# Two transformer blocks on one core: ScalarE makes the statistics of the first batches' normalizations and evicts the conditioning, the first batches get due times of their own, and two unread products run first

## The chip, the core and the metric

The kernel runs on one core of a Trainium2 chip. A core has TensorE (matrix products, "PE" in the profile), VectorE ("DVE"), ScalarE ("ACT"), GpSimd ("POOL") and SyncE ("SP", which here only issues DMAs). Each engine runs its own instructions strictly in the order in which they were written, and waits at semaphores for the others. The metric is device microseconds of one execution. Before the change the median of 3 runs is 1350.14 us (1349.22 to 1350.87).

## The reference

There are 16 batches of 256 tokens with 256 channels, all in fp32. Every batch goes through two blocks; the shapes in brackets are those of one batch.

```
c = silu(cond)                                   # per batch, 256
m = c @ w_ada + b_ada                            # 9 rows of 256: shift, scale, gate, three times
# block 0
h = ln(x) * (1 + m1) + m0;  q, k, v = split(h @ w_qkv + b_qkv)
    attention in two windows of 128, rolled by 64, 16 heads of 16       -> x += (o @ w_so + b_so) * m2
h = ln(x) * (1 + m4) + m3;  q = h @ w_q + b_q;  k, v = split(ctx @ w_kv + b_kv)
    scores 256 x 256 a head; the 16 largest of each row alone are kept,
    softmax over them                                                   -> x += (o @ w_co + b_co) * m5
h = ln(x) * (1 + m7) + m6;  a, b = split(h @ w_m1 + b_m1)               # 1024 each
    x += ((silu(a) * b) @ w_m2 + b_m2) * m8
# block 1
q from ln(x) * (1 + s1) + t1,  k, v from ln(ctx) * (1 + s2) + t2, where s, t = c @ Wss + bss
    attention over 256 keys                                             -> out = x + o @ Wp + bp
```

`ln` subtracts the mean of a row of 256 and divides by the root of its variance (with an epsilon). A batch has five of them: before the self attention, the top-k attention and the feed forward part (on x), and two in the last block, on the context and on x. What the change touches is how `ln`'s mean and variance are made for some batches, which engine takes the conditioning (m, s, t) out of the matrix product, and the order of everything.

## The kernel before, in words

Tokens lie on the 128 partitions, so that a batch is two tiles of 128 x 256. The pieces of a batch carry tags: `self` (self attention), `prep` (the context's keys and values and the queries for the top-k attention), `topk` (the top-k attention in four rounds of 4 x 2 heads), `mlp` and `last`; what is made once, such as weights, biases and conditioning, is tagged `start`.

Nothing runs in the order of the source. Each helper records operations with `op(engine, cost, emit, ...)`, that is, with the buffers that they read and write. Every operation has a due time: its batch plus an entry of the table `DUE` divided by 1000. The entry is found by the tag and by a running number within the tag. Tags of the first and the last batches have a number of their own (`self0`, `prep1`, `mlp15`), where that table entry stands for one batch alone; `self`, `prep`, `topk`, `mlp` and `last` serve all others. `Plan.order` sorts all operations by due time, assigns buffers, and writes the instructions out in this order, so a single list sets the order on all engines and on the DMA queue. It also estimates times from the given costs, with which it decides one thing: where TensorE would stand idle for over 1 us it puts in `filler` products (L353), one to two products of the identity that nobody reads.

The steps that the change touches:

- `normalized` (L436): VectorE makes the statistics with two `bn_stats` and two `bn_aggr` (L442, L444), GpSimd makes the reciprocal root and the negated mean in three small operations (L449 to L451), and then the normalized tile in two (L454). TensorE turns the result (L466), and ScalarE scales and shifts it while it copies it out (L480).
- `ada_columns` (L714): a piece of a weight of 256 KB is loaded (`rest<-in_L_xcond_w_ada_dram`, L711), multiplied with the conditioning (L721), and VectorE adds the bias from `bcol` as it copies the product out (L727, L729: two instructions of 128x16). There are 10 such pieces.
- `topk_round`: four score banks (L845), on each of which VectorE runs `max`, `match_replace`, `max`, `match_replace` for two heads (L864, L872, L884, L889), ScalarE the exponentials (L877), GpSimd the product of both (L893); then TensorE turns the weights (L542) and multiplies them with the values (L598).
- `lower`: 16 DMAs of 1 KB (L622) bring the negated maxima into the queries before the second scores (L806, L962).

The stationary layouts of TensorE differ: 128 x 128 for the big products, 32 rows at a time for the scores, and 17 columns for the weighted values (L598).

Of the kernel before, what the change touches and what calls it, by code (L numbers as in the profile page):

```python
# [10 lines left out]
F32 = mybir.dt.float32  # L11
# [5 lines left out]
P = 128  # L17
# [17 lines left out]
        -9079, -9474, -9247, -7795, -10959, -5686, -7231, -10933, -5595, -5764, -7671, -10944, -8055, -6777, -10987,  # L35
        -8081, -7859, -719, -437, -438, -481, -6999, -7280, -511, -720, -536, -6808, -436, -8602, -467, -7346, -144,
        -528, -1472, -8696, -179, -78, -9103, -26, -462, -493, -574, -8606, 35, 199, -2104, 292, -47, 992, 1098, 1338,
        -644, 26, -8994, -144, 52, 10, -8772, -241, -8701, 551, 74, 19, 1012, -516, -8708, 29, 1085, 1257, -514, -452,
        -6996, 1627, 1833, 1607, 911, 1468, 582, -843, -8601, 1445, 486,
    ),  # L40
    "self0": (
        -199, -1161, -7107, -1119, -1199, -1060, -1485, -9186, -125, -11006, -9245, -9080, -1563, -9248, -3868, -1470,
        -9200, -1606, -6831, -7277, -7299, -7349, -1217, -6958, -8697, -6883, -8698, -8665, -312, -310, -2158, -3486,
        -3338, -3035, -3750, -1684, -9048, -7290, -1182, -7290, -2158, -3339, -3752, -3826, -3561, -128, -8903, -9100,
        -1236, -8924, 9, -4022, -51,
    ),
    "prep0": (
        -524, -3251, -614, -3532, -3488, 354, -2949, 516, -8780, -39, -37, 80, 196, -3410, 569, -100, -3471,
    ),
    "topk0": (  # L50
        338, 282, 143, 7, -2799, -24, 100, -98, -2853, -35, 73, -8610, -2853, -8623, 112, -8616, -3052, -8436, -261,
        148, 579, -3006, -8621, -8749, 142, 439, -2809, 383, 324, 558, 726, -3356, -8631, -8719, 484, 172, -2951, 700,
        959, 1002, 919, 1061, 392, -8453, 550, -8714, -3364, 156, -461, 619, -3499, -8620, 551, 18, -2986, -61, 600,
        525, 700, 764, 725, 748, 690, -3352, 906, 842, 826, 553, 724, -72, 621, 835, 742, -3579, 803, 913, 816, 1073,
        821, 1081, 1074, 1309, 1219, 1329, 523, 620, 786, 1012, -3363, 1018, 801, 909, -3366, 958, 747, 1071, -3580,
        914, 791, 1170, -3634, 1022, 1024, 929, 1074, 820, 1013, 1016, 882, 1086, 819, 1181, 1178, 1255, 1240, 907,
        1133, 1169, 1256, 1239, 356, 1199, 1303, 1172, 1160, 1328, 1014, 1043, 1101, 1277, -3653, 1038, 1200, 1248,
        409, 1104, 1256, 1284, 352, 1060, 1143, 1107, 820, 1126, 1125, 1086, 972, 1307, 1262, 1260, 1197, 1206, 350,
        1052, 1246, 1188, 1311, 44, 1162, 1262, 1203, 1208, 1113, 1319, 1173, 1303, 1217, 1329, 677, 1356, 1398, 1437,
    ),  # L60
    "self1": (
        -4802, -987, -890, -482, -9103, -2047, -2146, -2225, -1549, -4844, -830, -1228, -5196, -3811, -1470, -4841,
        -4773, -861, -3828, -878, -800, -795, -794, -10252, -1021, -10208, -10029, -9854, -9854, -780, -807, -1214,
        -647, -4386, -4386, -4444, -3942, -602, -1053, -474, -328, -94, -659, -4237, -4066, -4401, -4387, -598, -1062,
        -270, -247, -15, 68, -4369, -213,
    ),
    "prep1": (
        -771, -5058, 71, -4579, -15, -331, -4364, 378, 34, 220, 223, 231, 182, -29, 145, 237, 302,
    ),
    "topk": (  # L70
        75, 3, 189, 110, 62, 3, -90, 2, 110, -39, 146, -53, -991, -146, 143, -62, -955, 353, 414, 558, 675, -104, 128,
        193, 253, 480, -914, 242, 339, 417, 490, -137, 393, 516, 407, 576, 134, 697, 349, 735, 402, 1049, 530, 279,
        443, -349, 556, 186, 562, 282, 1, 362, 587, 185, 11, 298, 611, 223, 479, 184, 179, 630, 712, -106, 253, 325,
        663, 746, 44, 673, 676, 706, 802, 580, 536, 739, 373, 857, 761, 882, 688, 894, 661, 942, 689, 837, 737, 833,
        885, 737, 799, 832, 902, 347, 344, 704, 30, 337, 331, 643, 725, 836, 941, 190, 1036, 1011, 826, 838, 232,
        1029, 960, 745, 776, 746, 903, 907, 736, 760, 415, 902, 909, 1090, 853, 1036, 1144, 1150, 894, 940, 677, 1028,
        721, 964, 206, 947, 922, 899, 675, 1026, 1075, 934, 678, 824, 918, 1039, 1051, 810, 1113, 1056, 691, 992, 779,
        1040, 959, 1033, 1027, 1116, 1109, 854, 1034, 1034, 999, 1107, 1008, 1160, 1027, 956, 1194, 1085, 501, 1236,
        1061, 1158,
    ),  # L80
    "self": (
        -1974, -677, -761, -758, -1718, -1767, -1387, -1242, -787, -1974, -758, -688, -1415, -1974, -694, -590, -601,
        -589, -1833, -538, -566, -1347, -1349, -1348, -345, -418, -466, -472, -473, -465, -226, -194, -253, -935,
        -969, -968, -425, -138, -335, -332, -197, -113, -150, -1139, -298, -295, -227, -133, -256, -227, -162, -70,
        -86, -126, -322,
    ),
    "prep": (
        -13, -197, -211, 5, 112, 57, 324, -19, -554, -568, -220, -220, -131, 617, 6, 17,
    ),
    "last": (  # L90
        1013, 1044, 1117, 1178, 1185, 1226, 6, 1311, 1060, 579, 1353, 1396, 2041, 1826, 1981, 1931, 2094, 1980, 2195,
        2146, 2088, 2131, 2195, 2090, 2231, 1173, 1171, 2258, 2182, 2188, 2187, 2280, 2286, 2324, 2285, 2351, 2342,
        2323, 2365, 2397, 2127, 2172, 2174, 2173, 2438, 2020, 2436, 1144, 1120, 1010, 1009, 2491, 2276, 2527, 2557,
        2522, 1882, 1284, 1283, 1388, 2589, 2220, 2310, 2627, 2557, 2593, 2591, 2133, 2518, 2425, 2647, 2528, 2649,
        2630, 2660, 2404, 2402, 2518, 2500, 2696, 2346, 2343, 2729, 2753, 2837, 2026, 2507, 2778,
    ),
    "mlp": (
        1668, 1326, 1271, 1268, 1484, 1490, 263, 1703, 1600, 1470, 1499, 1559, 1526, 1674, 1632, 1661, 1535, 959, 187,
        1556, 1289, 1565, 387, 1576, 1568, 1509, 398, 1568, 1257, 1602, 1505, 1616, 1614, 1238, 1421, 1717, 1041,
        1735, 1238, 1735, 1861, 1881, 1096, 1599, 1507, 1509, 1880, 1847, 1806, 859, 1648, 1897, 1712, 1861, 1529,  # L100
        1236, 1674, 882, 881, 1669, 1488, 1497, 847, 1474, 1745, 1088, 1027, 1748, 1027, 1396, 1020, 1336, 1944, 1978,
        1824, 2000, 1827,
    ),
    "self15": (
        -1762, -523, -14014, -616, -1736, -1651, -1652, -1042, -1147, -1738, -740, -1095, -1898, -709, -1266, -1267,
        -714, -1266, -347, -461, -328, -681, -998, -682, -328, -692, -173, -199, -712, -536, -370, -134, -249, -135,
        -196, -91, -162, -473, -302, -550, -648, -122, -354, -338, -167, -311, -83, -133, -766, -1659, -1733, -391,
# [1006 lines left out]
```

## Time and profile before

| what | value |
|---|---|
| median of 3 runs | 1350.14 us |
| profiled execution | 1350.46 us, its span 1348.6 us |
| PE busy | 1323.5 us (98%) |
| DVE busy | 1217.5 us (90%) |
| ACT busy | 1014.2 us (75%) |
| POOL busy | 1020.9 us (76%) |
| instructions in the span | 38673 |
| DMA | 42.45 MB, 31 GB/s in the mean |

The span runs from the first to the last instruction; the time holds some 1.9 us around it. The profile's windows give, for a stretch of the span, how long each engine was busy, the clock that TensorE was granted (1.00 is full speed) and what the DMA engines moved. A batch returns every 78.97 us in the middle of the span: the first score product of a top-k round of batches 3, 4 and 5 starts at 255.2, 334.2 and 413.2 us.

### The profile page before, as it was taken

Reading aid. Unit: us, or ns where it says so; the run is one execution under the profiler, and the core shown is the slowest. Engines: PE = TensorE matmul, PEld = TensorE weight load, DVE = VectorE, ACT = ScalarE, POOL = GpSimd, SP = SyncE. Lnnn points to the kernel's source line nnn. Section 1 sums busy time; section 2 is a strip of 40 time slices with the busy share of each in tenths; the row PEclk is TensorE's granted clock in tenths of the full one; section 3 lists DMA queues with packets and bytes.
Section 4 is the critical chain, followed back from the end, with each engine's and each line's share of the span. In section 5 each row is a group of like instructions: output and inputs, shape, how many; then the busy total and the mean of one; then the engine's idle time right before and its main releaser. Section 6 shows DMA issues by size and latency. Waiting matters only on the chain.

```text
span 1348.6 us, 38673 instructions
## 1 busy us (share of the span) xinstructions
PE 1323.5 (98%) x13494; PEld 1033.3 (77%) x13494; DVE 1217.5 (90%) x4358; ACT 1014.2 (75%) x2359; POOL 1020.9 (76%) x1552
## 2 busy tenths in 40 slices
PE   8889999999999999999999999999999999999998
PEld 6557787878778787887878788787878778787785
DVE  4699999999999999999999999999999999998844
ACT  4356779787887978778787777878777787978774
POOL 1377887879688787968878796887869788877962
PEclk9889999999999999999999999999999999999999
DMA  5430010101001010100101010010101000000000
GB/s 157 139 109 10 26 41 11 41 17 33 18 18 41 11 40 18 34 17 19 41 11 38 20 34 18 18 41 11 38 20 34 18 27 17 18 18 2 17 2 18
DMA packets 64161, 42.45 MB, mean 31 GB/s; under 512 B 37763, under 2 KB 56751, under 8 KB 63711
## 3 DMA queue, kind: packets, MB, share of 16 engines
q1 hardware_dynamic: 63967, 39.99, 10.7%
q8 instruction: 107, 1.75, 0.6%
q14 instruction: 87, 0.71, 0.2%
HBM read 35.14 MB, written 4.29 MB: 29 GB/s over the span
## 4 chain that ended last, share of the span: by engine, by line
PE 92%; DVE 3%; SPq 1%; issue 1%; DMA 1%; ACT 1%; POOL 0%; POOLq 0%; DVEq 0%; ACTq 0%
PE W L906 17%; PE W L492 12%; PE W L598 11%; PE W L542 8%; PE W L933 8%; PE W L528 6%; PE W L575 6%; PE W L950 5%; PE W L845 5%; PE W L962 5%; PE W L466 3%; PE W L806 2%; PE W L798 2%; SPq L622 1%; DVE rest L872 1%
## 5 line engine op out<-in xcount | busy, mean ns | idle before, releaser
L893 POOL TENSOR_TENSOR prT<-rest,prT 128x512 f32<-128x512 f32 x256 | 325.0, 1273 | 75.0 <-DVE rest L889 73.5
L605 DVE TENSOR_REDUCE nm<-W 128x2 f32<-128x512 f32 (+1 forms) x384 | 239.9, 682 | 30.9 <-PE W L798 17.4
L877 ACT ACTIVATE prT<-W,ntop 128x256 f32<-128x256 f32 x512 | 214.2, 491 | 52.2 <-POOL ntop L866 38.8
L906 PE MATMUL W<-xT,w_L_xcond_w_m 128*128 128x256 f32 (+1 forms) x1088 | 249.1, 373 | 0.0
L629 ACT ACTIVATE pTO<-W 128x512 f32<-128x512 f32 (+1 forms) x392 | 198.8, 596 | 41.9 <-PE W L962 28.9
L906 PEld LDWEIGHTS W<-xT,w_L_xcond_w_m 128*128 128x128 f32 x1088 | 187.6, 190 | 52.3 <-ACT pTO L629 10.6
L872 DVE MATCH_REPLACE8 rest<-top,W 128x256 f32<-128x256 f32 x512 | 209.0, 419 | 0.0
L889 DVE MATCH_REPLACE8 rest<-top,rest 128x256 f32<-128x256 f32 x512 | 206.7, 416 | 0.0
L864 DVE MAX8 top<-W 128x8 f32<-128x256 f32 x512 | 190.1, 420 | 15.7 <-PE W L845 12.8
L884 DVE MAX8 top<-rest 128x8 f32<-128x256 f32 x512 | 190.7, 418 | 0.0
L545 ACT ACTIVATE pTT<-W 128x512 f32<-128x512 f32 x256 | 148.7, 622 | 17.2 <-PE W L542 15.2
L542 PE MATMUL W<-ident,prT 128*128 128x128 f32 x1024 | 145.2, 277 | 4.4 <-ACT k L514 1.7
L542 PEld LDWEIGHTS W<-ident,prT 128*128 128x128 f32 x1024 | 117.9, 142 | 27.9 <-issue 6.2
L923 POOL TENSOR_TENSOR mb<-ma,mb 128x256 f32<-128x256 f32 (+1 forms) x136 | 94.8, 697 | 40.1 <-ACT mb L921 24.4
L558 POOL TENSOR_TENSOR on<-tr,rec 128x128 f32<-128x128 f32 (+1 forms) x162 | 71.0, 443 | 67.8 <-DVE rec L557 67.5
L933 PE MATMUL W<-w_L_xcond_w_m,h 128*128 128x256 f32 x512 | 113.7, 379 | 0.0
L933 PEld LDWEIGHTS W<-w_L_xcond_w_m,h 128*128 128x128 f32 x512 | 97.0, 190 | 13.7 <-POOL x L416 0.3
L555 DVE STREAM_TRANSPOSE tr<-W 128x256 f32<-128x256 f32 (+1 forms) x162 | 78.4, 485 | 29.6 <-PE W L598 15.6
L598 PE MATMUL W<-pTO,v 128*17 128x128 f32 (+1 forms) x2112 | 102.2, 323 | 0.0
L926 POOL TENSOR_TENSOR h<-h,mb 128x256 f32<-128x256 f32 (+1 forms) x136 | 94.7, 696 | 8.2
L416 POOL TENSOR_TENSOR x<-x,gated 128x512 f32<-128x512 f32 (+1 forms) x49 | 60.4, 1233 | 40.9 <-ACT gated L415 40.9
L921 ACT ACTIVATE mb<-W,half 128x256 f32<-128x256 f32 (+1 forms) x136 | 64.4, 489 | 31.7 <-PE W L906 31.6
(129 smaller groups left out, 2678.5 us busy)
## 6 DMA issues: line engine op xcount, KB each, us to landing
gate<-gates SPq DMA_DIRECT2D x48, 256.0 KB
q<-nmT SPq DMA_DIRECT2D x480, 1.0 KB
cx<-in_ctx_dram SPq DMA_DIRECT2D x19, 256.0 KB
cx<-in_ctx_dram SPq DMA_DIRECT2D x104, 32.0 KB
rest<-in_L_xcond_w_ada_dram SPq DMA_DIRECT2D x9, 256.0 KB
x<-in_x_dram SPq DMA_DIRECT2D x16, 128.0 KB
x<-in_x_dram SPq DMA_DIRECT2D x32, 64.0 KB
w_L_xcond_w_m<-in_L_xcond_w_m_dram SPq DMA_DIRECT2D x1, 2048.0 KB
```

What stands on the lines that cost most here:

```text
L542: nc.tensor.transpose(w.t[:, ts(n, P)], flat[:, ts(n, P)], ident)
L598: nc.tensor.matmul(po.t[ds(NW * j, DH + 1), ds(q0, nq)], v.t[:, kt, 8 * m + 2 * j + a, :], pT.t.rearrange("p n q -> p (n q)")[:, ds(part, ...
L605: op("DVE", 0.61, lambda j=j, s=s: nc.vector.tensor_reduce(nm.t[:, k, ds(j, groups, step=4)], s.t.rearrange("p (g k) -> p g k", g=groups), ...
L629: op("ACT", 0.24 + q * 0.0005, lambda s=s, pT=pT: nc.scalar.activation(pT.t.rearrange("p n q -> p (n q)")[:, :q], s.t[:, :q], AF.Exp), r=[ ...
L864: nc.vector.max(top.t[:, a, 0:8], s.t[:, ts(a, L)])
L872: nc.vector.match_replace(rest.t[:, a, :], top.t[:, a, 0:8], s.t[:, ts(a, L)], TAKEN)
L877: nc.scalar.activation(pr.t[:, a, :], s.t[:, ts(a, L)], AF.Exp, bias=ntop.t[:, a:a + 1])
L884: nc.vector.max(top.t[:, a, 8:16], rest.t[:, a, :])
L889: nc.vector.match_replace(rest.t[:, a, :], top.t[:, a, 8:16], rest.t[:, a, :], TAKEN)
L893: op("POOL", 1.25, lambda: nc.gpsimd.tensor_tensor(pr.t, rest.t, pr.t, ALU.mult), r=[rest, pr], w=[pr])
L906: nc.tensor.matmul(w.t[:, :q], w_m1.t[:, c, ds(n0, P)], xT.t[:, c, :q], start=c == 0, stop=c == NCC - 1)
L933: nc.tensor.matmul(pp.t[:, ts(k, C)], hs[f].t[:, ts(k, P)], w_m2.t[:, f, :], start=f == 0, stop=f == NHC - 1)
```

## The change

1. `normalized` gets a second way, `by_scalar`: ScalarE adds up each tile (an Identity into a tile `unread` with `accum_out`), GpSimd turns the sum into the negated mean, ScalarE squares with this mean as the bias and adds up again, and GpSimd makes the root. Seven normalizations take it: the self attention's and the top-k attention's of batches 1 and 2, and for batch 0 the feed forward's and both of the last block.
2. `ada_columns` has its products taken out by ScalarE. For the scales a second copy of the biases, `bcol1`, holds the bias plus one.
3. `self2`, `prep2`, `topk1`, `mlp0`, `mlp1`, `last0` and `last1` become tags of their own, and all due times are new.
4. Two products of a tile of ones (`warmed`), which nobody reads, stand first on TensorE. VectorE sets this tile as its first instruction, and makes the head masks a little later in the source.
5. The plan's DMA rate (`RATE`, in KB per us) is 250 instead of 320, which changes its estimates, and with them where fillers stand and which buffers are taken.

```
-ISSUE, BEGIN, LAND, RATE, OPEN = 0.53, 0.9, 0.4, 320.0, 8
+WARM = 2
+ISSUE, BEGIN, LAND, RATE, OPEN = 0.53, 0.9, 0.4, 250.0, 8
...
+    unread = const.tile([P, C], F32, name="unread")
...
+    nc.vector.memset(tiles["rest"][-1], 1.0)
...
+    def warmed():
+
+        z, w = tiles["rest"][-1].rearrange("p a l -> p (a l)"), tiles["W"][-1]
+        for _ in range(WARM):
+            nc.tensor.matmul(w, z[:, :P], z, start=True, stop=True)
...
-    def normalized(x, eps, tt):
-
-        st, mv, xn, n = Buf("st"), Buf("mv"), Buf("xn"), len(tt)
+    def normalized(x, eps, tt, by_scalar=False):
+
+
+        mv, xn, n = Buf("mv"), Buf("xn"), len(tt)
+        if by_scalar:
+            def added():
+                for k, t in enumerate(tt):
+                    nc.scalar.activation(unread, x.t[:, t, :], AF.Identity, accum_out=mv.t[:, k, 0:1])
+            op("ACT", 0.08 + 0.45 * n, added, r=part(x, tt), w=[mv])
+            op("POOL", 0.25, lambda: nc.gpsimd.tensor_scalar(mv.t[:, :n, 2], mv.t[:, :n, 0], -1.0 / C, None, ALU.mult), r=[mv], w=[mv])
+
+            def squares():
+                for k, t in enumerate(tt):
+                    nc.scalar.activation(unread, x.t[:, t, :], AF.Square, bias=mv.t[:, k, 2:3], accum_out=mv.t[:, k, 1:2])
+            op("ACT", 0.08 + 0.45 * n, squares, r=[*part(x, tt), mv], w=[mv])
+
+            def root():
+                m = mv.t[:, :n, 1]
+                nc.gpsimd.tensor_scalar(m, m, 1.0 / C, eps, ALU.mult, ALU.add)
+                nc.gpsimd.tensor_tensor(m, m, neg_half[:, :n], ALU.pow)
+            op("POOL", 0.8 + 0.16 * n, root, r=[mv], w=[mv])
+            return scaled(x, xn, mv, tt)
+        st = Buf("st")
...
-    bcol = fixed("bcol", [P, total])
+    bcol, bcol1 = fixed("bcol", [P, total]), fixed("bcol1", [P, total])
...
-        op("DVE", 0.2, lambda: nc.vector.tensor_copy(bcol.t[:, ds(first, total)], w.t[:, :total]), r=[w],
-           w=[(bcol, names is first_biases)])
+        def emit():
+            nc.vector.tensor_copy(bcol.t[:, ds(first, total)], w.t[:, :total])
+            nc.vector.tensor_scalar(bcol1.t[:, ds(first, total)], w.t[:, :total], 1.0, None, ALU.add)
+        op("DVE", 0.35, emit, r=[w], w=[(bcol, names is first_biases)])
...
-                if plus_one:
-                    nc.vector.tensor_scalar(dst.t[:, m, :], pm.t[:, ds(m * P, B)], col(bias, chunk + m), 1.0, ALU.add, ALU.add)
-                else:
-                    nc.vector.tensor_scalar(dst.t[:, m, :], pm.t[:, ds(m * P, B)], col(bias, chunk + m), None, ALU.add)
-        op("DVE", 0.32, out_of_it, r=[pm, cols(bias)], w=[dst])
+                c = col_of[bias] + chunk + m
+                nc.scalar.activation(dst.t[:, m, :], pm.t[:, ds(m * P, B)], AF.Identity, bias=(bcol1 if plus_one else bcol).t[:, c:c + 1])
+        op("ACT", 0.6, out_of_it, r=[pm, cols(bias)], w=[dst])
...
-        xT = channel_major(normalized(x, EPS0, tt), nt, 0, b)
+        xT = channel_major(normalized(x, EPS0, tt, b in (1, 2)), nt, 0, b)
...
-        xT = channel_major(normalized(x, EPS0, tt), len(tt), 1, b)
+        xT = channel_major(normalized(x, EPS0, tt, b in (1, 2)), len(tt), 1, b)
...
-        xT = channel_major(normalized(x, EPS0, tt), nt, 2, b)
+        xT = channel_major(normalized(x, EPS0, tt, b < 1), nt, 2, b)
...
-        cT = channel_major(normalized(load_cx(b), EPS1, BOTH), NT, "kv", b)
+        cT = channel_major(normalized(load_cx(b), EPS1, BOTH, b < 1), NT, "kv", b)
...
-        xT = channel_major(normalized(x, EPS1, tt), nt, "q", b)
+        xT = channel_major(normalized(x, EPS1, tt, b < 1), nt, "q", b)
...
-        alone = {"self": (0, 1, B - 1), "prep": (0, 1, B - 1), "topk": (0, B - 1)}.get(name, (B - 2, B - 1))
+        alone = {"self": (0, 1, 2, B - 1), "prep": (0, 1, 2, B - 1), "topk": (0, 1, B - 1)}.get(name, (0, 1, B - 2, B - 1))
...
     with tc.manual_schedule():
+        warmed()
         plan.run()
```

The table `DUE` itself (all its numbers differ) is left out, and so is the moved block of the masks.

## The prediction

> **What bounds the kernel now.** I read the page first (busy times, slices), then the windows of five stages, then who waited for whom, then the time line where engines stood idle.
>
> ```profile
> PE 1323.5 (98%) x13494; PEld 1033.3 (77%) x13494; DVE 1217.5 (90%) x4358; ACT 1014.2 (75%) x2359; POOL 1020.9 (76%) x1552
> PE   8889999999999999999999999999999999999998
> DVE  4699999999999999999999999999999999998844
> PEclk9889999999999999999999999999999999999999
> ...
> 0.00:56.00 56.00, 48.82 (x438) 35.23 (x438) 26.98 (x93) 21.99 (x44) 13.61 (x32) 1.00 0.54 162
> 56.00:160.00 104.00, 93.03 (x874) 68.22 (x874) 98.04 (x391) 67.80 (x157) 75.09 (x112) 0.92 0.18 55
> 160.00:256.00 96.00, 96.00 (x916) 76.78 (x912) 91.78 (x338) 72.79 (x167) 78.73 (x118) 1.00 0.11 30
> 256.00:1045.00 789.00, 789.00 (x8200) 623.49 (x8199) 752.25 (x2681) 622.49 (x1430) 633.28 (x943) 1.00 0.10 26
> 1045.00:1348.60 303.60, 296.62 (x3078) 229.57 (x3078) 248.44 (x859) 229.11 (x564) 220.22 (x351) 1.00 0.06 15
> ```
>
> The windows' columns are: stretch, its length, busy time of PE, PEld, DVE, ACT and POOL, granted clock, DMA share, GB/s. From 160 to 1045 us PE is busy for every microsecond, so there only PE's own work counts, and a batch takes 78.97 us. From 56 to 160 us it is otherwise: DVE is busy for 98.0 of 104 us and PE for 93.0, of which some are fillers. This is the first top-k attention: its four rounds take DVE 46 us, and PE has too little other work. Up to 56 us neither is full: a chain through loads, conditioning and the first self attention.
>
> ```profile
> 3.97 2.08 PE L353 MATMUL W<-ident 128*128 128x512 f32 x2
> 10.50 1.02 PE L353 MATMUL W<-ident 128*128 128x512 f32 x2
> 58.96 3.78 PE L353 MATMUL W<-ident 128*128 128x512 f32 x4 [3.54 <-ACT prT L877]
> ...
> 92.79 0.76 DVE L442 BATCH_NORM_STATS2 st<-cx 128x6 f32<-128x256 f32 x2
> 93.44 0.32 DVE L444 BATCH_NORM_AGGREGATE mv<-st 128x2 f32<-128x6 f32 x2
> 103.07 0.38 DVE L727 TENSOR_SCALAR ada_scale_kv<-W,bcol 128x16 f32<-128x16 f32 x2
> ...
> 393.57 1.94 PE L598 MATMUL W<-pTO,v 128*17 128x128 f32 x64
> 395.33 1.06 PE L598 MATMUL W<-pTT,v 128*17 128x128 f32 x32
> 396.31 1.14 PE L845 MATMUL W<-k,q 32*128 32x512 f32 x8
> ```
>
> ```profile
> 56.00:58.00 2.00, 0.00 (x0) 0.00 (x0) 2.00 (x10) 0.00 (x0) 1.83 (x6) 0.88 0.01 2
> 76.00:78.00 2.00, 2.00 (x7) 1.21 (x6) 2.00 (x11) 0.06 (x1) 2.00 (x5) 0.50 0.00 0
> 102.00:104.00 2.00, 2.00 (x6) 1.56 (x6) 2.00 (x9) 0.12 (x1) 2.00 (x3) 0.50 0.32 90
> ```
>
> The time line gives start and length. The filler takes 2.08 us at 3.97 and 1.02 us at 10.50: PE runs at half speed until about 10 us. Windows of 2 us (below, granted clock third from the end) show three more halved stretches, by the traced clock 57.8 to 64.6, 74.8 to 81.6 and 102.1 to 105.5 us, 17 us in all. The rows at 92.79 to 103.07 are DVE work that the change takes away, in the middle of the stretch in which DVE is full. The last three rows price a change of the stationary layout: two L598 lots start 1.76 us before the third, 0.88 each, while the third, with L845 behind it, takes 0.98 to the next start. So a change costs 0.10 us.
>
> **The sum, part by part.** All terms are against the profiled execution (1350.46 us, span 1348.6), which is 0.32 us above the median.
>
> 1. *DVE work taken out of the full stretch.* Of the seven statistics, those of the first self attentions ran at 11.39 and 51.33 us, where DVE had holes, and two at 166.64 and 174.33, where PE is full; these four give nothing. Three lie in the stretch: 92.79 to 93.76 (0.97), 94.54 to 95.47 (0.93), 126.08 to 127.05 (0.97), together 2.87 us. Of the ten conditioning pieces four do: 103.07 (0.38), 121.99 (0.33), 130.26 (0.37) and 153.88 (0.38), together 1.46. That is 4.33 us, and PE can follow DVE by as much: in 56 to 160 it is idle for 10.97 us and spends 6.95 on fillers (3.78, 1.13, 1.02, 1.02). I take -4.3. Bounds: 0, if the waits grow by as much, and -10.3, if the 5.96 us in which DVE stands idle there go too (its longest, 1.41 us at 67.1, follows the slow fillers at 58.96).
> 2. *What ScalarE gets.* Seven times four passes over a 128x256 tile; the nearest row, h<-h at L925, takes 0.46 us: 12.9 us. Twenty evictions of 128x16, between the 0.20 us of the 128x1 activation and the 0.42 of the 16x256 one: 4 to 8.4. ACT is busy for 67.8 of 104 us in the full stretch and would reach about 76. On GpSimd three small operations stay three (0.22, 0.70 and 0.25 at 46.06). The way gets longer: DVE's 0.97 becomes twice 0.92 on ACT with a GpSimd step of 0.24 between and two more handoffs of 0.1, so +1.3 us each. Behind the waiting square stand the exponentials of L877 and L629, which TensorE's L542 and L598 await. In the written order the sums of context 0 and of batch 2 stand together and their squares ten instructions later, so there the wait is covered by evictions; for the other five the squares follow at once or after one step. I take 0, covered by PE's other work, with 2.6 (batch 1 before its queries, batch 0 before the feed forward part) as the upper bound and 0 as the lower, since a longer way saves nothing.
> 3. *The two unread products.* DVE sets the 128x512 tile first; 128x256 took 0.27 us, so some 0.5 from 0.8. Then two products at the cold price of 2.08, to about 5.5. The conditioning's transpose (3.68) falls behind them, the copy of 0.18 follows, and the first conditioning product (6.43, held there by its biases' DMA until 6.23) comes about 1 us late, but PE has then worked without a break, and may be at full speed where it ran cold before: the first sixteen took 3.80 us, the later eights 1.06 each, so 1.7 us come back. I take -0.3, between +1.0 and -1.0.
> 4. *The way to the first top-k round* (first max at 55.43). PE waited 1.44 us at 44.7 for a 256 KB piece; in the new order that product stands behind both lots of the first scores of batch 1. Against this, a 2 MB weight is now issued ahead of batch 1's gate row and maxima DMAs: in 64 to 72 us 2 MB moved at 161 to 430 GB/s, so 5 to 8 us. But these 16 issues are in two lots of 8 now, and took 9.5 us at 51.57. On DVE the second bias copy, 2 x 0.2, lies in holes. I take 0, between -2 and +2.
> 5. *The clock.* In the first 130 us the program holds 4 fillers in place of 10, and the rows count a busy filler as work. Each window of 3.41 us (57.8 to 64.6 is two) at half speed loses 1.7 us of PE work, which counts only where PE then has a backlog. I take half a window more, +0.9; bounds two fewer, -3.4, and three more, +5.1.
> 6. *The order.* A middle batch changes the layout 30 times in place of 31: ten batches x 0.10 = -1.0. Before batch 3 there are 85 in place of 79, half of them in the full stretch: +0.3. At the end one fewer: -0.1. Between no wait and one wait of 0.4 us in every batch (the longest wait of PE from 160 us to the end of the full middle): -1.5 to +3.0.
> 7. *The end* (1045 to 1348.6) has the same operations and two fillers more in places that were idle: 0, bounds -1.5 and +1.5.
>
> Sum: -4.3 + 0 - 0.3 + 0 + 0.9 - 0.8 + 0 = -4.5. 1350.46 - 4.5 = 1345.96, and 0.32 less against the median: **1345.6 us**.
>
> *A rule against it.* The trace dropped to half speed at 57.8 after a hole from 55.4 to 59.0, and at 74.8 after nothing longer than 1.03 us, only with PE thin in that window. The Trainium skill (TensorE: Matmul & The Clock Gate, "HAM oscillation — how this bites in real kernels") says to leave no hole over some 3.4 us. By the rule, only the hole at 55.4 would matter, and taking out fillers from shorter holes would be free, so term 5 would be 0 and the sum -5.4; the trace's second drop disagrees.
>
> **The rivals.**
>
> *No change, by the clock.* With fewer fillers PE is thin in more windows, and the backlog of the feed forward part of batch 0 runs at half speed. Three windows more (5.1 us) in place of my half (0.9) turn -4.5 into -0.3: about 1349.8. For it: the drop at 74.8 without a hole. Against it: the ten fillers of before prevented none of the three drops, so the drops are near their limit in any order; and the new order has self attention products of batch 2 between the top-k rounds of batch 0, where fillers stood.
>
> *Slower, by a wait that returns in every batch.* The new middle order puts two L598 lots of the last block side by side, the second of which needs four exponentials of 0.60 us more, and GpSimd and DVE are at 80% and 95% there. A wait of w costs 10 w: above 0.45 us nothing of the gain is left, above 0.72 us the kernel is over the bound of slower; at 1.0 us it takes 1355.6. For it: the middle has no slack on PE at all. Against it: the old middle shows no wait over 0.4 us with nearly the same order and the same other engines.
>
> *More.* DVE's idle time shrinks with the fillers at 58.96 gone (-1.4), and one halved stretch of two windows vanishes (-3.4 in place of +0.9): 1345.6 - 5.7 = 1339.9.
>
> *It doesn't do what it says.* If ScalarE's accumulation cost much more than a plain pass, say twice the 0.46, ACT would get 13 us more, 5.5 of them in the full stretch, where it has 36 us free; so this alone gives no more than the 2.6 of term 2, 1348.2.
>
> **How the numbers follow.** The forecast gets 0.57, no change by the clock 0.18, slower by a wait 0.13, more 0.08, a costly accumulation 0.04. Within 0.2% (2.7 us, about what a measurement of this kernel can tell) of 1350.14 is 1347.4 to 1352.8. The forecast's own range, from the bounds that are not rivals (terms 3, 4 and 7: +-1.0, 2 and 1.5, by the root of their squares 2.7, with some rounding 3), is 1342.6 to 1348.6, so nine tenths of it are faster: 0.52, with "more" 0.60, and two in a hundred of the costly accumulation make 0.62. Within the bound are the rest of these and the clock rival, 0.25; slower 0.13. The range takes in the clock rival above, half of "more" below, and leaves out the returning wait: 1341 to 1351.5.
>
> **What would show it.** Right: DVE's L442 and L727 gone from 56 to 160 us and that stretch some 4 us shorter, the first score product of batch 3 at 251 in place of 255.2; batches 78.87 us apart in the middle; PE full from 160 us on; the filler near 10 us no slower than now, the first conditioning products 1.06 an eight. Wrong: PE windows at half speed between 100 and 135 us with L906 in them; a wait of PE in the middle that shows once a batch; ACT's squares waiting for GpSimd with L877 behind them; the first max of the top-k attention after 57 us. The sum fails if DVE does not stay the bound of the stretch.

## The result and the profile after

The changed kernel takes 1357.09 us (median of 5 runs, 1355.81 to 1357.55) against 1350.86 of the kernel before in the same session: a ratio of 1.0043, with a 95% interval of 1.0029 to 1.0058. It is slower by 0.43%, where 0.33% faster was forecast. The profiled execution took 1357.55 us, its span 1355.8 us, 7.2 more than before. One execution among all of these, the profiled one of the fifth experiment, took 3366.91 us, far from the other nine of its kernel; its time and its profile are left out.

First come the page's busy times, then the windows of the same stretches as before (stretch, its length, busy time of PE, PEld, DVE, ACT and POOL, granted clock, DMA share, GB/s).

```profile
PE 1328.1 (98%) x13490; PEld 1031.1 (76%) x13490; DVE 1208.5 (89%) x4313; ACT 1029.1 (76%) x2435; POOL 1024.8 (76%) x1552
```

```profile
0.00:56.00 56.00, 51.58 (x450) 36.60 (x451) 24.66 (x80) 30.66 (x80) 18.14 (x40) 1.00 0.52 165
56.00:160.00 104.00, 95.62 (x895) 71.03 (x894) 99.00 (x388) 77.58 (x194) 77.24 (x114) 0.93 0.20 57
...
256.00:1045.00 789.00, 781.99 (x8108) 614.85 (x8108) 742.54 (x2643) 611.61 (x1411) 626.96 (x931) 1.00 0.10 25
```

DVE has 9 us less to do in the whole and ACT 15 us more, as the change says. What is new stands in the last row: from 256 to 1045 us PE was busy for all 789 us before, and now for 782.

The batches tell the same by place. The table gives the first score product (L845 before, L930 after) of the first top-k round of some batches, from the traces, and the mean step from batch 3 to batch 13:

| kernel | batch 0 | 1 | 2 | 3 | 13 | step, 3 to 13 | from 13 to the end |
|---|---|---|---|---|---|---|---|
| before | 54.3 | 110.3 | 176.0 | 255.2 | 1044.9 | 78.97 | 303.8 |
| after | 53.6 | 109.6 | 172.1 | 250.3 | 1050.6 | 80.03 | 305.2 |

So the beginning won 4.9 us, almost the forecast ("at 251 in place of 255.2"). Then ten batches lost 10.6 us, and the end 1.4 (of which 1.3 in one more such batch: 80.51 us from 13 to 14, against 79.18): -4.9 + 10.6 + 1.4 = +7.1. The single steps of the middle are no longer alike: 79.50, 79.51, 82.73, 79.39, 80.6, 79.67, 81.13, 79.2, 79.37, 79.2.

Who waited for whom between 256 and 1045 us (engine and line, releaser: us in total, times, longest); in the kernel before neither the row on L627 nor the one on the context had a counterpart:

```profile
PE W L627 <- ACT xT L565: 5.4, 5, 1.8
...
SPq L707 <- DVE nmT L700: 322.4, 30, 22.5
SPq L456 <- POOL gated L492: 105.4, 9, 12.5
...
DVE st L524 <- DMA cx<-in_ctx_dram: 12.3, 9, 2.6
```

VectorE waits in nine batches of ten for the load of the last block's context. The time line of one of them, around the first score product of batch 5 at 409.3 us (start, length, engine, line, what it made from what, and in brackets the idle time before it and who ended it):

```profile
406.24 0.33 SPq L456 DMA_DIRECT2D gate<-gates  x1
406.66 0.39 SPq L436 DMA_DIRECT2D cx<-in_ctx_dram  x1
...
412.07 0.76 DVE L524 BATCH_NORM_STATS2 st<-cx 128x6 f32<-128x256 f32 x2 [2.52 <-DMA cx<-in_ctx_dram]
...
412.96 2.07 DVE L949 MAX8 top<-W 128x8 f32<-128x256 f32 x6
413.80 0.21 POOL L951 TENSOR_SCALAR ntop<-top 128x2 f32<-128x2 f32 x1 [2.37 <-DVE top L949]
...
414.05 0.84 ACT L962 ACTIVATE prT<-W,ntop 128x256 f32<-128x256 f32 x2 [2.81 <-POOL ntop L951]
414.77 1.02 ACT L565 ACTIVATE xT<-W,ada_shift_q,ada_scale_q 128x256 f32<-128x256 f32 x2
...
415.94 1.51 PE L627 MATMUL W<-ident,prT 128*128 128x128 f32 x8 [1.74 <-ACT xT L565]
```

Read it upward. PE stands for 1.74 us because ACT's `xT` is late. That instruction has had its input since about 412 (PE turned it at 411.38), but on ACT it stands behind the exponentials, which wait for GpSimd's negated maxima, which wait for DVE's `max`, which stands behind the statistics of the context, which wait for a DMA issued at 406.66. Nobody needs these statistics yet; they are only first in a queue. And the DMA is late because on SP it stands behind the load of a gate row, which waits up to 12.5 us for its buffer, one of three, until GpSimd has used the row that lies in it (at L492, which ended at 406.21). In the kernel before the two stood the other way round:

```profile
405.63 0.39 SPq L374 DMA_DIRECT2D cx<-in_ctx_dram  x1
406.12 1.73 SPq L368 DMA_DIRECT2D x<-in_x_dram  x3
410.08 0.33 SPq L394 DMA_DIRECT2D gate<-gates  x1
...
412.33 0.72 DVE L442 BATCH_NORM_STATS2 st<-cx 128x6 f32<-128x256 f32 x2
```

There the load leaves 7.6 us ahead of the batch's first score product (413.2), now 2.7 us ahead (409.3). It took 5.4 us from issue to the statistics (406.66 to 412.07). Gate rows waited for their buffers in the kernel before as well, between 256 and 1045 us:

```profile
SPq L394 <- POOL x L401: 132.2, 20, 9.0
...
SPq L394 <- POOL gated L430: 21.9, 10, 2.2
```

But VectorE waited for no context load there, so these waits held back nothing that was needed in time.

That reading of the two traces is the theory: *the gate row ahead of the context load on SP, with three buffers for all gate rows, costs the 10.6 us of the middle*. Its rivals: the new order on TensorE, the new work of ScalarE and GpSimd, or the two transfers hindering each other.

### The profile page after: what moved, and what is told of

The parts are those of the page before. It is cut to its first block, busy times and chain, and to the rows that moved or that the text cites. A ratio compares the mean times of both kernels' runs of the same rounds, so it can differ in the third digit from the quotient of the medians.

```text
span 1355.8 us, 38612 instructions
## 1 busy us (share of the span) xinstructions
PE 1328.1 (98%) x13490; PEld 1031.1 (76%) x13490; DVE 1208.5 (89%) x4313; ACT 1029.1 (76%) x2435; POOL 1024.8 (76%) x1552
## 4 chain that ended last, share of the span: by engine, by line
PE 75%; DVE 11%; POOL 3%; DMA 2%; ACT 1%; issue 1%; SPq 0%; POOLq 0%; DVEq 0%
PE W L991 17%; PE W L577 9%; PE W L683 9%; PE W L627 7%; PE W L1018 5%; PE W L660 5%; PE W L1047 5%; PE W L1035 4%; PE W L613 4%; PE W L930 4%; DVE rest L957 2%; DVE top L949 2%; PE W L891 2%; POOL prT L978 2%; PE W L883 2%; PE W L551 2%
## 5 line engine op out<-in xcount | busy, mean ns | idle before, releaser
L962 ACT ACTIVATE prT<-W,ntop 128x256 f32<-128x256 f32 x512 | 211.2, 499 | 80.2 <-POOL ntop L951 57.7
L991 PEld LDWEIGHTS W<-xT,w_L_xcond_w_m 128*128 128x128 f32 x1088 | 190.2, 192 | 42.4 <-ACT pTO L714 10.6
L949 DVE MAX8 top<-W 128x8 f32<-128x256 f32 x512 | 188.0, 416 | 14.5 <-PE W L930 12.9
L969 DVE MAX8 top<-rest 128x8 f32<-128x256 f32 x512 | 185.9, 409 | 0.0
L627 PE MATMUL W<-ident,prT 128*128 128x128 f32 x1024 | 148.6, 279 | 11.5 <-ACT xT L565 6.7
L630 ACT ACTIVATE pTT<-W 128x512 f32<-128x512 f32 x256 | 153.1, 622 | 2.1 <-PE W L627 2.0
L627 PEld LDWEIGHTS W<-ident,prT 128*128 128x128 f32 x1024 | 114.7, 141 | 49.5 <-POOL ntop L951 10.2
L683 PEld LDWEIGHTS W<-pTO,v 128*17 128x17 f32 x2112 | 53.8, 98 | 40.1 <-DVE rest L974 8.3
```

The lines of the kernel that those rows point to most:

```text
L627: nc.tensor.transpose(w.t[:, ts(n, P)], flat[:, ts(n, P)], ident)
L683: nc.tensor.matmul(po.t[ds(NW * j, DH + 1), ds(q0, nq)], v.t[:, kt, 8 * m + 2 * j + a, :], pT.t.rearrange("p n q -> p (n q)")[:, ds(part, ...
L949: nc.vector.max(top.t[:, a, 0:8], s.t[:, ts(a, L)])
L962: nc.scalar.activation(pr.t[:, a, :], s.t[:, ts(a, L)], AF.Exp, bias=ntop.t[:, a:a + 1])
L969: nc.vector.max(top.t[:, a, 8:16], rest.t[:, a, :])
L991: nc.tensor.matmul(w.t[:, :q], w_m1.t[:, c, ds(n0, P)], xT.t[:, c, :q], start=c == 0, stop=c == NCC - 1)
```

## The experiments

### 1. The context load ahead of the gate row again

One due time of the changed kernel is altered.

```
     "last": (
-        1090, 985, 1173, 1133, 1130, 1208, ...
+        850, 985, 1173, 1133, 1130, 1208, ...
```

> The changed kernel, with one due time altered (the load of the last block's context, 1090 to 850), so that SP issues this load right after the x load and ahead of the gate row, as the kernel before does. Nothing else in the order of any engine moves in the middle. Theory (the context load stands behind the gate row, whose buffer waits for GpSimd; it lands late, VectorE's statistics wait for it 2.5 us and TensorE gets its transposes late): the statistics no longer wait, TensorE shows no wait on ACT's xT in the middle, batches there take about 78.9 us in place of 80.0, the gain of the beginning (first score product of batch 3 at 250.3) stays, and the time is 1345 to 1347 us, under both kernels. Rival A (the new order on TensorE, or ScalarE's and GpSimd's new work, lengthens each batch): batches stay at about 80.0 us and the time at 1356 to 1358. Rival B (half of it is the order): 1350 to 1353.

Measured: 1346.15 us (11 runs, 1345.10 to 1347.79), ratio to before 0.9975 (0.9966 to 0.9984). SP's rows of its time line for the same batch (first score product at 408.0), and the window of the middle:

```profile
390.58 2.33 SPq L430 DMA_DIRECT2D x<-in_x_dram  x3
393.01 0.54 SPq L436 DMA_DIRECT2D cx<-in_ctx_dram  x1
404.93 0.33 SPq L456 DMA_DIRECT2D gate<-gates  x1
```

```profile
256.00:1045.00 789.00, 788.04 (x8191) 622.22 (x8190) 748.83 (x2676) 620.14 (x1429) 634.81 (x941) 1.00 0.10 26
```

The gate row still waits for its buffer, but nothing is behind it that anyone is short of. One thing more moved than was expected: the statistics of the context, which could not stand ahead of their load, now stand ahead of those of x on VectorE (at 397.91 and 406.85 us; in the changed kernel at 412.07 and 407.60). So this experiment alone does not tell the place of the load from the place of its statistics; the next one does. The step falls from 80.03 to 79.10 us, batch 3 starts at 249.6, and the kernel beats the one before. The rivals that leave 1350 or more fall. A little is left over, since the step was to be 78.9:

```profile
489.56 0.31 PEld L551 LDWEIGHTS W<-ident,xn 128*128 128x128 f32 x3 [0.28 <-POOL xn L539]
```

This row is from its time line, 2.5 us behind the first score product of the batch that starts at 487.1. With the context's ahead of them, the statistics of x start 1.1 us ahead of the batch's first score product (1.7 in the second experiment, below), and TensorE waits 0.3 us a batch for GpSimd's `xn`.

### 2. A fourth gate buffer, the order left alone

```
-            ... "gate": (3, [P, 2, C]), "nm": (4, [P, NT, 32]), "nmT": (4, [P, NT, 32]),
+            ... "gate": (4, [P, 2, C]), "nm": (4, [P, NT, 32]), "nmT": (3, [P, NT, 32]),
```

> The changed kernel with four gate buffers in place of three (and three in place of four for the transposed maxima). SP's order in the middle is that of the changed kernel, the gate row ahead of the context load; but the gate row has a second buffer there and need not wait for GpSimd. Theory (the wait for the buffer holds the context load): SP no longer waits at the gate row, the context lands in time, batches take about 78.9 us and the time is 1345 to 1348 us. Rival A (the transfers of gate row and context hinder each other, whatever SP waits for): the context still lands late, 1355 to 1358. Rival B (order on TensorE): no change, 1356 to 1358.

Measured: 1342.44 us (4 runs, 1340.59 to 1343.24), ratio to before 0.9947 (0.9934 to 0.9961): better than the 1345 to 1348 expected, and the fastest complete kernel of this study. By the traces every engine and SP's queue run the same instructions in the same order as in the changed kernel; only buffers differ. The gate row stands ahead of the context load as in the changed kernel, but no longer waits; both leave 14 us ahead of the batch's first score product (405.2). The time line, and the window of the middle:

```profile
390.39 0.58 SPq L456 DMA_DIRECT2D gate<-gates  x1
391.06 0.39 SPq L436 DMA_DIRECT2D cx<-in_ctx_dram  x1
...
405.36 0.70 DVE L524 BATCH_NORM_STATS2 st<-cx 128x6 f32<-128x256 f32 x2
```

```profile
256.00:1045.00 789.00, 789.00 (x8231) 624.41 (x8220) 753.99 (x2692) 623.10 (x1435) 637.95 (x946) 1.00 0.10 26
```

PE is full again, and the step is 78.75 us, under that of before (78.97). So the order of TensorE did not cost anything: with nothing in its way it gains 0.22 us a batch. Nor does it matter, with 14 us in hand, that two transfers stand side by side. Whether the gate row's transfer lengthens the context's where it is late, these runs do not separate.

### 3. The fault put into the kernel before

Its gate row gets an earlier due time, so that it stands ahead of the x load and the context load.

```
     "self": (
-        -1974, -677, -761, -758, -1718, ...
+        -1974, -677, -997, -758, -1718, ...
```

> The kernel before, with one due time altered (the gate row, -761 to -997), so that SP issues the gate row ahead of the x load and the last block's context load in the middle; nothing else changes there. Theory: the old order gets the fault of the new one, VectorE's statistics wait for the context load in every batch, batches take 80 to 82 us in place of 78.97, and the time is 1360 to 1380 us. Rival (the place of the context load doesn't matter; the order on TensorE does): 1349 to 1352 us.

Measured: 1371.63 us (4 runs, 1369.54 to 1375.68), ratio 1.0171 (1.0152 to 1.0190). The time line of the batch whose first score product is at 417.2:

```profile
414.14 0.33 SPq L394 DMA_DIRECT2D gate<-gates  x1
414.56 0.39 SPq L374 DMA_DIRECT2D cx<-in_ctx_dram  x1
...
418.53 0.75 DVE L442 BATCH_NORM_STATS2 st<-cx 128x6 f32<-128x256 f32 x2 [2.06 <-DMA cx<-in_ctx_dram]
```

Batch 3 starts at 255.3, as before, and the step becomes 80.84 us: 10 x 1.87 = 18.7 us from one due time, without any of the change; by the traces only SP's order differs from the kernel before.

### 4. Both factors crossed: the gate row first, and four buffers

The third experiment's kernel with the second's buffers.

> The third experiment's kernel (the kernel before, with the gate row issued ahead of the x load and the context load; 1371.6 us) with the second experiment's buffers (four gate buffers, three for the transposed maxima). It crosses the two factors in the old order. Theory (what costs is the wait for the gate row's buffer at the head of SP's queue, not the order as such): the wait falls away, the context lands in time, batches are 78.97 us apart again and the time is 1348 to 1351 us. Rival (the gate row's transfer ahead of the context's, or the later x load, costs by itself): batches stay above 80 us and the time above 1360.

Measured: 1349.28 us (10 runs, 1348.28 to 1353.33), ratio 0.9997 (0.9987 to 1.0007). SP's rows of its time line:

```profile
400.51 0.58 SPq L394 DMA_DIRECT2D gate<-gates  x1
409.11 0.39 SPq L374 DMA_DIRECT2D cx<-in_ctx_dram  x1
409.60 1.66 SPq L368 DMA_DIRECT2D x<-in_x_dram  x3
```

The gate row now leaves 8.6 us before the context load, which goes out 7.2 us ahead of the batch's first score product (416.3), as in the kernel before. The step is 78.99 us, and PE is busy for all of the middle. The order costs 22 us with three gate buffers and nothing with four; so it is the wait at the head of the queue, and not the order, that costs.

### 5. Four buffers in the kernel before

> The kernel before with the same change of buffers as the second experiment (four gate buffers, three for the transposed maxima), nothing else. It tells whether that experiment's lead over the kernel before (1342.4 against 1349.7) belongs to the change or to the buffers. Theory: before, the context load already stands ahead of the gate row, nothing on TensorE waits in the middle, so the fourth buffer gives nothing there: batches stay 78.97 us apart and the time is 1348 to 1351 us. Rival (a gate row that never waits also lets the loads of the beginning come earlier, whatever the order): 1343 to 1347.

Measured: 1349.88 us (9 runs, 1346.98 to 1351.44), ratio 0.9990 (0.9980 to 0.9999). There is no profile of it to use, so the step of its batches is not shown. In the old order the fourth buffer is worth at most 0.2%, and the second experiment's lead over the kernel before, 0.53%, is more than the buffer alone.

### 6. The statistics back on VectorE

The first experiment's kernel; the sums become `bn_stats` and `bn_aggr`, the squares fall away.

```
-            def added():
-                for k, t in enumerate(tt):
-                    nc.scalar.activation(unread, x.t[:, t, :], AF.Identity, accum_out=mv.t[:, k, 0:1])
-            op("ACT", 0.08 + 0.45 * n, added, r=part(x, tt), w=[mv])
+            st = Buf("st")
+            def stats():
+                for k, t in enumerate(tt):
+                    nc.vector.bn_stats(st.t[:, k, :], x.t[:, t, :])
+                for k in range(n):
+                    nc.vector.bn_aggr(mv.t[:, k, 0:2], st.t[:, k, :])
+            op("DVE", 0.04 + 0.43 * n, stats, r=part(x, tt), w=[st, mv])
...
```

> The first experiment's kernel (context load ahead of the gate row) with the seven statistics that ScalarE makes given back to VectorE (two bn_stats and two bn_aggr each, in the place of the sums), under the same due times. Theory (the beginning is bound by VectorE, and what is taken out of the stretch from 56 to 160 us is gained): the first score product of batch 3 is later than in the first experiment by about 2.9 us, the three statistics that lie in the stretch, and the time is longer by as much, about 1348 to 1350 us. Rival (the gain of the beginning comes from the new order and not from VectorE's lighter load): within 1 us of the first experiment.

Measured: 1354.88 us (4 runs, 1353.58 to 1355.21), ratio 1.0040 (1.0026 to 1.0053). Against the first experiment's 0.9975 that is 0.65%, 8.8 us, three times the expected. The middle is the same (79.05 us a batch); batch 3 starts at 257.2 instead of 249.6. From batch 0's first score product to batch 2's it takes 124.2 us instead of 118.0, that is 6.2 us more, and in between stand four of these lots on VectorE, 3.26 us of `bn_stats` and 1.38 of `bn_aggr`. The rest is waiting. Its time line shows one long hole of TensorE:

```profile
124.38 1.21 PE L930 MATMUL W<-k,q 32*128 32x512 f32 x1 [5.85 <-DVE nm L690]
```

VectorE is late with the row maxima there. So VectorE's load counts in this stretch, and the rival falls. The size is not the price of the work alone: the places of these instructions were chosen for ScalarE, which probably makes it an upper bound, but no run has better places.

### 7. The statistics left out of the kernel before

```
         def stats():
+            if left_out:
+                nc.vector.memset(mv.t, 1.0)
+                return
```

> The kernel before, in its own order, with the seven statistics that the change gives to ScalarE left out (VectorE sets the tile to a constant in their place, so those normalizations scale by a constant and the outputs differ from the reference's). It measures the relief of VectorE alone, without the new order and without ScalarE's work. Theory (VectorE bounds 56 to 160 us): the first score product of batch 3 comes 2.9 us (the three lots in the stretch) to 5 us earlier than the 255.2 of the kernel before, and the time falls by as much, to 1345 to 1347 us. Rival (the waits grow by as much, the gain of the beginning comes from the new order): within 1 us of 255.2 and of 1349.7.

Measured: 1348.25 us (10 runs, 1347.40 to 1352.47), ratio 0.9987 (0.9975 to 0.9999), that is, 1.8 us less with an interval of 0.1 to 3.4. In the profile batch 3 starts at 253.0, 2.2 earlier (in an execution that ran at half speed for 3.4 us only, against 17.1 in the profile before, so that this is no clean measure either). This is less than the 2.9 of the theory and more than the rival's none. So in the old order VectorE's relief is worth some 2 us, and in the new one its absence costs up to 9: what the relief is worth depends on the order, and it has no price of its own.

### 8. The conditioning back on VectorE

The second experiment's kernel with `op("DVE", 0.32, ...)` and `tensor_scalar` in `ada_columns`.

> The second experiment's kernel with the ten conditioning pieces evicted by VectorE again, in the places that they have on ScalarE now; the order of everything else is the same. Theory (VectorE bounds the beginning; four of the ten pieces lie in its full stretch, 1.46 us): the first score product of batch 3 comes 1.5 to 2.4 us after the second experiment's 247.8, the middle is the same 78.75 us a batch, and the time is 1344 to 1345 us. Rival (this part of the change brings nothing, the holes take it): within 0.5 us of the second experiment, 1342 to 1343.

Measured: 1346.90 us (6 runs, 1346.09 to 1348.43), ratio 0.9969 (0.9957 to 0.9981) against 0.9947: 0.22%, some 3 us (4.5 by the medians), more than the theory's range. The middle has the same 78.75 us a batch. In the profile batch 3 starts at 255.2, 7.4 us after the second experiment's 247.8, where 1.5 to 2.4 were expected; the two executions differ in the clock as well, at half speed for 17.1 us here before batch 3 and for 10.2 there. Beside VectorE's 1.46 us and the clock another effect shows: one piece now stands in VectorE's queue among the `max` and `match_replace`, and TensorE waits for it. This is a row of TensorE's waits between 53 and 120 us:

```profile
PE W L891 <- DVE ada_scale_kv L814: 1.0, 1, 1.0
```

These do not add up to 7.4 us; the rest stays open.

### 9. No unread products

The second experiment's kernel with `WARM = 0`.

> The second experiment's kernel without the two products at the beginning that nobody reads; all else is the same. Theory (term 3 of the prediction, -0.3 between +1.0 and -1.0): TensorE reaches full speed some 2 us later, and the first score product of the first top-k attention comes 0 to 1 us later than the second experiment's 52.9; the time is 1342 to 1343.5 us. Rival (they stand in the way of the first conditioning products): the first score product comes 0.5 to 1 us earlier and the time is 1341.5 us.

Measured: 1343.59 us (4 runs, 1342.64 to 1345.05), ratio 0.9941 (0.9925 to 0.9958) against 0.9947 (0.9934 to 0.9961). No difference can be told. In the profiles full speed comes at 12.5 us instead of 4.7, and the first score product at 55.5 instead of 52.9; but these are the slowest execution of the one kernel and the fastest of the other, so the 2.6 us are no measure. That full speed comes earlier is seen elsewhere too: at 4.7 to 7.6 us in the six profiles with the two products, at 8.3 to 13.1 in the five without.

### 10. What ScalarE's part costs

The second experiment's kernel without the statistics: a single small activation sets a constant in the place of the sums, nothing stands for the squares.

```
             def added():
-                for k, t in enumerate(tt):
-                    nc.scalar.activation(unread, x.t[:, t, :], AF.Identity, accum_out=mv.t[:, k, 0:1])
+                nc.scalar.activation(mv.t[:, :n, 0:2], x.t[:, tt[0], 0:2 * n].rearrange("p (k a) -> p k a", a=2), AF.Exp, scale=0.0)
...
             def squares():
-                for k, t in enumerate(tt):
-                    nc.scalar.activation(unread, x.t[:, t, :], AF.Square, bias=mv.t[:, k, 2:3], accum_out=mv.t[:, k, 1:2])
+                pass
```

> The second experiment's kernel (1342.4 us) with the seven statistics left out on ScalarE as well: one small activation writes a constant in the place of the sums and nothing stands in the place of the squares, so those normalizations scale by a constant and the outputs differ from the reference's. Order and GpSimd's steps stay. It measures what ScalarE's part costs on the way (term 2 of the prediction: 0, at most 2.6 us). Theory (covered by TensorE's other work): the time is within 0.7 us of the second experiment's, 1341.7 to 1343.1. Rival (the longer way of these normalizations is on the path): the first score product of batch 3 comes 1.5 to 3 us earlier than 247.8 and the time is 1339.5 to 1341.

Measured: 1341.09 us (4 runs, 1340.56 to 1341.61), ratio 0.9929 (0.9912 to 0.9945). The two intervals overlap; by the medians it is 1.35 us, by the ratios 2.4. Batch 3 starts at 247.8 in both profiles, though this one ran at half speed for 13.6 us before that and the second experiment's for 10.2. The time lies between the ranges of theory and rival; the place of batch 3 speaks for the theory. So the new way of the seven normalizations costs between nothing and 2.4 us, and which of these stays open.

## Why the prediction was wrong, step by step

**What bounds the kernel: right.** In the middle PE alone bounds the kernel as long as its inputs come in time, and in the beginning VectorE's load counts (experiments 6 and 7). This is also why a wait of a microsecond in the middle counts ten times.

**Term 6, the order: this step failed.** It gave -0.8, with "no wait" and "one wait of 0.4 us in every batch" as its bounds; the middle alone cost +10.6. It held TensorE's instructions of a middle batch against the old ones, counted the layouts, and took the bound of a new wait from the longest wait in the old trace. That wait of 0.4 us lies behind 1045 us, in the end; from 160 to 1045 us PE of the kernel before waits for nothing, so the figure bounded nothing. (Ten times 0.4 on top of -0.8 would also be +3.2, not +3.0.) The due times order all queues, SP's among them. The step that would have shown it was to read SP's queue for one batch in both orders: the context load goes from ahead of the x load and the gate row to behind both, and the waits already say what a gate row waits for, its buffer. What it did count had the right sign: without the wait the new order saves time in the middle, 0.22 us a batch instead of the 0.10 forecast (experiment 2). That a change of layout is what saves it is not shown.

**The rival "slower, by a wait that returns in every batch": right in kind, wrong in place.** It priced a wait w at 10w and gave 1355.6 for 1.0 us; the loss turned out as 1.07 us a batch (with 1.7 us that the clock took once in the ten, last section) and the time as 1357.1. It looked for it at two L598 lots and their exponentials. It was a load held in SP's queue, four queues away from the hole on PE. Against it stood the old middle "with nearly the same order", which holds for TensorE and was not looked at for SP. And the range of 1341 to 1351.5 left this case out.

**Term 1, VectorE's work taken out (-4.3).** The beginning gained 4.9 us in the profile after, 5.6 in the first experiment's. That this is so close to the forecast is in part luck: in the old order the relief by the statistics gives only 1.8 us (experiment 7), in the new one it is worth up to 8.8 (experiment 6) and the conditioning some 3 to 4.5 more (experiment 8). The count of VectorE's microseconds in the stretch isn't the price where order and load act together.

**Term 2, ScalarE (0, at most 2.6).** Within the bounds: 0 to 2.4 (experiment 10). These are the groups of instructions of the kernel after (busy us, mean ns of one):

```profile
L511 ACT ACTIVATE unread<-x,mv 128x256 f32<-128x256 f32 x12 | 6.1, 509 | 1.6 <-POOL mv L507 1.4
L505 ACT ACTIVATE unread<-x 128x256 f32<-128x256 f32 x12 | 5.1, 423 | 2.9 <-POOL x L478 1.6 <-DMA x<-in_x_dram 1.0
...
L505 ACT ACTIVATION_READ_ACCUMULATOR unread<-x 128x1 f32 x12 | 2.3, 195 | 0.0
L511 ACT ACTIVATION_READ_ACCUMULATOR unread<-x,mv 128x1 f32 x12 | 2.3, 188 | 0.0
...
L511 ACT ACTIVATE unread<-cx,mv 128x256 f32<-128x256 f32 x2 | 1.0, 508 | 0.1
L505 ACT ACTIVATE unread<-cx 128x256 f32<-128x256 f32 x2 | 0.8, 417 | 1.2 <-DMA cx<-in_ctx_dram 1.1
```

There are 28 passes, as counted, and they take 13.0 us, as forecast (12.9). What the prediction left out is an instruction of 0.19 us behind each of them that fetches the sum and that begins before the pass has ended: with these ScalarE is busy for 15.6 us, 0.56 for a pass with its fetch. The rival of a costly accumulation, twice the 0.46, was thus too dear. The evictions were taken at 0.20 to 0.42 us; they take 0.27.

**Term 3, the unread products (-0.3).** No difference measured, in keeping with it (experiment 9). The step went as described: in the profile after, the first conditioning product starts 0.9 us later (7.33 instead of 6.43), and an eight of them takes 1.16 us from the start.

**Term 4, the way to the first top-k round (0).** It comes 0.7 us earlier (53.6 instead of 54.3), within the bounds.

**Term 5, the clock (+0.9): open.** By the traced clock the kernel before ran at half speed for 17.1 us between 57.5 and 105.3 (the prediction reads the three stretches 0.2 to 0.3 us too late), the one after for 13.6 us in its beginning (69.0 to 72.4 and 116.8 to 127.0): one window of 3.4 us fewer, not half a window more. But executions of one and the same kernel differ by more than that (last section), so one profile of each does not give the sign. The price of 1.7 us for a window was probably too dear: the last section has about 0.5. The rival "no change, by the clock" falls, since batch 3 came 4.9 us earlier and the loss is elsewhere.

**Term 7, the end (0).** It took 1.4 us more, within its bound of 1.5, but 1.3 of this is the middle's wait once more, from batch 13 to 14; without that wait the end takes 303.6 us (experiment 2) against 303.8.

With the middle's wait gone, the forecast's -4.5 is about what is seen: experiment 1 lies 0.25% under the kernel before, 3.4 us, and experiment 2, without the remaining wait for `xn`, 0.53%, 7.2 us. That the forecast lies between them is partly luck, since terms 1 and 6 do not have the sizes that it gave them.

## What to carry to other kernels

When a change gives new due times, compare every queue in both orders for one turn of the steady part, DMA queues first: a load that has to wait for its buffer holds all loads behind it, and a hole on the busiest engine can have its cause four queues away. Bound a new wait by what the thing waits for (the time until its buffer comes free, up to 12.5 us here), not by the waits that the old order shows. And price a wait in the steady part by the number of turns before looking at gains in the beginning: a microsecond there undid all that the change had won, and one more buffer gave it back.

## What the runs showed of the hardware that was not expected

The clock fell once in the middle of the changed kernel, at 417.2 us, for 3.4 us, right after the hole of 1.74 us that ended at 415.94:

```profile
414.00:416.00 2.00, 0.26 (x2) 0.09 (x2) 2.00 (x9) 1.95 (x5) 2.00 (x4) 1.00 0.01 4
416.00:418.00 2.00, 1.86 (x10) 1.53 (x11) 1.97 (x10) 2.00 (x6) 1.84 (x5) 0.79 0.00 0
418.00:420.00 2.00, 2.00 (x6) 1.56 (x6) 2.00 (x10) 0.48 (x1) 1.83 (x5) 0.50 0.02 4
```

PE's busy time is the second number of each row, the granted clock the third from the end. Eight projection products at 417.25 took 3.54 us, where such an eight takes 1.89 at full speed (the time line of the first experiment, 482.21). The hole and the 1.7 us lost by the halved clock make up the 3.3 us by which that batch's step of 82.73 us is longer than most of its neighbours (79.4). In the third experiment PE waits in every batch, for at most 0.9 us at a time, and the clock holds at full speed through the whole middle. The Trainium skill (TensorE: Matmul & The Clock Gate, "HAM oscillation — how this bites in real kernels") warns of holes of over some 3.4 us; here one of half that length was followed by the lower clock, so the rule's bound is too wide for this case. The length of a hole alone does not decide either: in the kernel before, one of nearly the same length was followed by full speed until 101.9 us.

```profile
94.28 0.63 PE L542 MATMUL W<-ident,prT 128*128 128x128 f32 x4 [1.68 <-ACT k L514]
```

The halved stretches of the beginning differ between executions more than the changes do: by the traces 17.1 us before, 13.6 in the third and the fourth experiment with nearly the same beginning, and 3.4 in the seventh. They come in multiples of 3.4 us. A single profile can thus not tell a microsecond or two in the beginning; the medians can.

What a halved stretch costs can be estimated from the times alone. Beside the experiments the kernel before ran 56 times, with a mean granted clock from 0.993 to 0.999, which is half speed for some 19 to 3 us of the span. The 22 runs at 0.993 took 1350.98 us in the mean, the seven at 0.999 took 1348.45: 2.5 us for some 16 us of half speed, about 0.5 us for a window of 3.4. This is a relation between runs; nothing varied the clock by itself. By the same rate some 1 us of what experiments 6 and 8 cost may be the clock's, as their runs have 0.992 to 0.995 and the kernels that they are compared with 0.994 to 0.996.
